# Accumulating layer 1's sums in PSUM, and reading layer 0's attention weights from PSUM

## The chip, the cores and the metric

The kernel runs on one core of a Trainium2 chip, as one launch, in float32. The metric is the device time of the launch in microseconds; lower is better. Five engines work side by side and meet at semaphores: PE (TensorE, matrix multiplies, with PEld for the loading of weights), DVE (VectorE), ACT (ScalarE), POOL (GpSimd) and SP (SyncE, which only issues transfers here). SBUF is the working memory on the chip[...].

## The reference

Two graph layers over 3327 nodes with 512 features; the adjacency matrix has about nine ones in a row. Each layer is added to its input and normalised over the features.

```python
# layer 0: attention with 4 heads of 128 features
feats = jnp.einsum('nf,hfo->hno', X, W)
logits = leaky_relu(e_s[:, :, None] + e_n[:, None, :], 0.2) + NEG_INF * (1.0 - A)
out = relu(einsum('hnm,hmo->hno', softmax(logits), feats) + b)   # heads side by side
x = layernorm(x + out)
# layer 1: a sparse attention and a plain graph convolution, each with a gate
attn_a = sigmoid(concat([adj @ x, x], axis=1) @ Wa.T + ba)       # attn_b with Wb, bb
h = x @ W_sa
e = where(adj != 0, exp(-leaky_relu(s_left[:, None] + s_right[None, :], 0.01)), 0)
x_a = (e / (sum(e, axis=1) + 1e-5)) @ h
x_b = adj @ (x @ W_gcnb) + b_gcnb
x = layernorm(x + sigmoid(attn_a * x_a + attn_b * x_b))
```

The biases are inputs and are added. A second pass over the dense matrix stands behind a branch for inputs that don't fit the sparse lists; it isn't taken here.

## The kernel before

Everything up to about 285 us reads the adjacency matrix, makes for each node the list of its neighbours (up to 24), sorts the nodes by degree into 26 tiles of 128 rows, and writes the rows of layer 0's features to a table in memory. The tiles have 4 to 14 neighbour slots (`CAPS`); the nodes of tiles 0 and 12 that have more share one extra gathered set of rows (`stair`), which two small matrices spread and join (`to_nodes`, L664, and `to_rows`, L676).

Both layers then loop over the 26 tiles. For each tile POOL issues one indirect transfer for each slot (`indirect`, L614, with the instruction on L615): 128 rows of 520 numbers from the table in memory into a ring of 42 slots in SBUF. `plan` lists the gathers of all tiles ahead, and `gather` issues as many as the ring has room for; a tile's slots are given back in `free`, when its readers are done. Other transfers of a loop are few: the scatters of finished rows, L146, also on POOL.

**Layer 0** (loop at L948). `weigh_a` and `weigh_b` make the attention weights of the next tile on DVE and ACT, as `w`, 25 slots by 4 heads. `attend` (L783) multiplies each gathered row by its slot's weights, head by head: DVE for two slots of three (L797, one instruction over 512 numbers, the four weights spread over 128 numbers each), ACT for the third (L795, four instructions). PE adds the rows up in a PSUM bank by multiplying with the identity (L803). `finish` (L883) adds the result to the row, then the norm's statistics follow.

**Layer 1** (loop at L1131). Each turn works on four tiles of the order: `j1` (next; its weights are made), `j` (its rows are summed), `jp` (projected), `jpp` (gated, added and measured). The queues run in the order that the loop writes them (`manual_schedule`), and each engine takes its own instructions in that order:

- `to_sbuf(jp, 1)`, `turn(jp)`, `to_sbuf(jp, 0)`: ACT copies the plain sum of `jp`, which PE has made already transposed (L1098), out of PSUM; PE transposes the weighted sum (L1107); ACT copies that (both copies L1112).
- `plain_sum(j)` on PE, and `weighted(j, 0)` on DVE: the first part of the weighted sum, one SCALAR_TENSOR_TENSOR a slot (L1085): sum = row x weight + sum, the sum `sw` in SBUF, begun by ACT with the tile's own row (`scaled_first`, L1070).
- For `jpp`: DVE adds the bias to the plain projection (L1147), multiplies by the gate and adds the other projection (L1148), and ACT takes the tanh (L1149).
- `project(jp, 1)` and `project(jp, 0)` on PE: the plain and the weighted sum through the two 512x512 matrices (L1118, four matmuls each).
- `weights_a(j1)` (L1032 to L1054), `weighted(j, 1)` (the rest of the slots, and L1087 with the joined rows' sum for tiles 0 and 12), finished rows' norm on ACT (L1161) and their scatters, the residual add of `jpp` (L1171), `weights_b(j1)` (L1059 to L1062), `scaled_first(j1)` (for tiles 0 and 12 with L1073 and the matmul L1075), and the statistics of `jpp` (L692).

Of the kernel before, what the change touches and what calls it, by code (L numbers as in the profile page):

```python
# [8 lines left out]
F32 = mybir.dt.float32  # L9
AF = mybir.ActivationFunctionType  # L10
ALU = mybir.AluOpType
# [13 lines left out]
S = 24  # L25
# [53 lines left out]
def sparse_pass(  # L79
# [104 lines left out]
    def row1(j):  # L184
        g, i = place(j)
        return x1[g][:, i, :]
# [551 lines left out]
        few, many = few[1:], many[1:]  # L738
    order0 += second[-1:]
    assert sorted(order0) == list(range(NT))  # L740
    ws, accs, ws2 = {}, {}, {}

    def weigh_a(j):
        c = slots(j)
# [25 lines left out]
            nc.scalar.copy(ids2[g], stair[j][:, F + H : F + H + 1])  # L770
        nc.scalar.copy(row1(j)[:, 0:F], got[j][0][2][:, 0, 0:F])

    def weigh_b(j):
        c, w = slots(j), ws[j]
        den = m0.tile([P, 1, H], F32, tag="den", name=f"den{j}")
        nc.vector.tensor_reduce(den[:, 0, :], w[:, :c].rearrange("p s h -> p h s"), AX.X, ALU.add)
        nc.vector.reciprocal(den, den)
        nc.vector.tensor_mul(w[:, :c], w[:, :c], den.to_broadcast([P, c, H]))
        if j in T0:
            small = psx.tile([P, B * H], F32, tag="pcol", name=f"to_rows{j}", bufs=2)  # L780
            ws2[j] = to_rows(m0, small, f"n{j}", w[:, C0 + 1 :, :])

    def attend(j, lean, between):  # L783


        w = ws[j]
        acc = accs[j] = ps.tile([P, F], F32, tag="acc", name=f"acc{j}", bufs=2)
        if not lean:
            nc.tensor.matmul(acc, ident, bias0, start=True, stop=False)
        for s0, n, buf, o in got[j]:  # L790
            for s in range(s0, s0 + n):
                gv = buf[:, o + s - s0, 0:F].rearrange("p (h o) -> p h o", h=H)
                if s % 3 == 2:
                    for h in range(H):
                        nc.scalar.activation(gv[:, h, :], gv[:, h, :], AF.Copy, scale=w[:, s, h : h + 1])  # L795
                else:
                    nc.vector.tensor_tensor(  # L797
                        gv, gv, w[:, s, :].rearrange("p (h o) -> p h o", o=1).to_broadcast([P, H, FO]), ALU.mult
                    )
                row = buf[:, o + s - s0, 0:F]  # L800
                if lean and s == 0:
                    nc.vector.tensor_add(row, row, bias0)  # L802
                nc.tensor.matmul(  # L803
                    acc, ident, row, start=(lean and s == 0), stop=(s == CAPS[j] and j not in T0)
                )
                if s == 2:
                    between()
        if j in T0:
            gv = stair[j][:, 0:F].rearrange("p (h o) -> p h o", h=H)
            nc.vector.tensor_tensor(  # L810
                gv, gv, ws2[j].rearrange("p (h o) -> p h o", o=1).to_broadcast([P, H, FO]), ALU.mult
            )
            nc.tensor.matmul(acc, to_node, stair[j][:, 0:F], start=False, stop=True)
# [116 lines left out]
    over = x1b.tile([P, NT, S], F32, name="over")  # L930

    psx = tc.alloc_tile_pool(name="psx", bufs=1, space=PSUM, side="right")
    psum = psx.tile([P, B * H], F32, tag="pcol", name="pv1sum", bufs=2)[:, :NCOL]
    for k in range(KT):
        nc.tensor.matmul(psum, ones, v1[:, k, :], start=(k == 0), stop=(k == KT - 1))
# [78 lines left out]
        order += long[:1] + short[:1]  # L1014
        short, long = short[1:], long[1:]
    order += last
    ew, gates, sums, plain, proj, zs, stair_sum = {}, {}, {}, {}, {}, {}, {}

    def own_score(j):
        ew[j] = m1.tile([P, S + 1], F32, tag="e", name=f"e{j}", bufs=3)  # L1020
        nc.scalar.copy(ew[j][:, 0:1], row1(j)[:, F + 6 : F + 7])

    def weights_a(j):
# [2 lines left out]
        e = ew[j]  # L1026
        gate = gates[j] = m1.tile([P, 12], F32, tag="gate", name=f"gate{j}", bufs=5)
        if j in T0:
            small = ps1.tile([P, B * H], F32, tag="small", name=f"to_nodes1_{j}")
            cols = to_nodes(m1, small, f"l1_{j}", stair[j][:, F : F + 3])  # L1030
        for s0, n, g, _ in got[j]:
            nc.vector.tensor_scalar(e[:, s0 : s0 + n], g[:, :n, F], row1(j)[:, F + 3 : F + 4], None, ALU.add)  # L1032
# [23 lines left out]
    def weights_b(j):  # L1056

        c, e, gate = slots(j), ew[j], gates[j]
        nc.vector.tensor_scalar(gate[:, 2:3], gate[:, 2:3], 1e-5, None, ALU.add)  # L1059
        nc.vector.tensor_scalar(gate[:, 0:2], gate[:, 0:2], 0.5, 0.5, ALU.mult, ALU.add)  # L1060
        nc.vector.reciprocal(gate[:, 2:3], gate[:, 2:3])
        nc.vector.tensor_scalar(e[:, :c], e[:, :c], gate[:, 2:3], gate[:, 0:1], ALU.mult, ALU.mult)  # L1062
        if j in T0:
            small = ps1.tile([P, B * H], F32, tag="small", name=f"to_rows1_{j}")
            ws2[j] = to_rows(m1, small, f"l1_{j}", e[:, C0 + 1 :].rearrange("p (b o) -> p b o", o=1))

    def scaled_first(j):

        sw = sums[j] = m1.tile([P, F], F32, tag="sw", name=f"sw{j}")
        nc.scalar.activation(sw, row1(j)[:, 0:F], AF.Copy, scale=ew[j][:, 0:1])  # L1070
        if j in T0:
            scaled = m1.tile([P, F], F32, tag="scaled", name=f"scaled{j}", bufs=1)
            nc.scalar.activation(scaled, stair[j][:, 0:F], AF.Copy, scale=ws2[j])  # L1073
            stair_sum[j] = ps1.tile([P, F], F32, tag="stair", name=f"stair_sum{j}")
            nc.tensor.matmul(stair_sum[j], to_node, scaled, start=True, stop=True)  # L1075

    def weighted(j, part):

        e, sw = ew[j], sums[j]
        cut = 2 + (CAPS[j] * 5 + 7) // 8  # L1080
        for s0, n, g, _ in got[j]:
            for i in range(n):
                s = s0 + i
                if (s < cut) == (part == 0):
                    nc.vector.scalar_tensor_tensor(sw, g[:, i, 0:F], e[:, s : s + 1], sw, ALU.mult, ALU.add)  # L1085
        if part == 1 and j in T0:
            nc.vector.tensor_add(sw, stair_sum[j], sw)  # L1087

    def plain_sum(j):

# [20 lines left out]
        sT = zs[j, half] = m1.tile([P, KT, P], F32, tag=f"sT{half}", name=f"sT{half}_{j}")  # L1111
        nc.scalar.copy(sT, (turned, plain)[half][j])  # L1112

    def project(j, half):
        sT, wt = zs[j, half], (wsa, wg)[half]
        po = proj[j, half] = ps1.tile([P, F], F32, tag=f"po{half}", name=f"po{half}_{j}", bufs=1 + half)
        for k in range(KT):
            nc.tensor.matmul(po, sT[:, k, :], wt[:, k, :], start=(k == 0), stop=(k == KT - 1))  # L1118

    ends = {3, 7, 11, 15, 19, 22, 24, 25}  # L1120
    norm = Norm(m1, "n1", ends)
# [9 lines left out]
    for i in range(NT + 3):  # L1131
# [3 lines left out]
        gather()  # L1135
        if j1 is not None:
            own_score(j1)
        if jp is not None:
            to_sbuf(jp, 1)
            turn(jp)  # L1140
            to_sbuf(jp, 0)
        if j is not None:
            plain_sum(j)
            weighted(j, 0)
        if jpp is not None:
            za = zs[jpp] = m1.tile([P, F], F32, tag="za", name=f"za{jpp}", bufs=3)
            nc.vector.tensor_add(za, bias_g, proj[jpp, 1])  # L1147
            nc.vector.scalar_tensor_tensor(za, za, gates[jpp][:, 1:2], proj[jpp, 0], ALU.mult, ALU.add)  # L1148
            nc.scalar.activation(za, za, AF.Tanh, scale=0.5)  # L1149
        if jp is not None:  # L1150
            project(jp, 1)
            project(jp, 0)
        if j1 is not None:
            weights_a(j1)
        if j is not None:
# [16 lines left out]
        if j1 is not None:  # L1172
            weights_b(j1)
            scaled_first(j1)
        if jpp is not None:
            ready = norm.add(i - 2, zs[jpp])

# [451 lines left out]
```

## Time and profile before

| what | value |
|---|---|
| median of 3 runs | 1068.92 us (1057.76 to 1071.53) |
| the profiled execution's own time | 897.77 us |
| its span, first to last instruction | 895.8 us |
| mean granted clock of TensorE | 0.908 |
| layer 0's loop | about 285 to 527 us |
| layer 1's first and last gather, issued at | 530.94 and 842.26 us |
| PE's last projection ends | 879.8 us |

A line of the groups is: source line, engine, operation, output<-inputs, shapes, count | busy us, mean ns of one | idle us of the engine just before them, and what ended it. The chain that ended last is followed back from the last instruction to what released each one. PE's clock is granted in full or by half, by the profile's rows. The profiled execution is shorter than the timed runs by 171 us.

### The profile page before, as it was taken

How to read it: one execution, taken by the hardware profiler on the slowest of the kernel's cores; microseconds unless marked ns; L12 is line 12 of the kernel's file. 1: busy time of each engine (PE TensorE's matmuls, PEld its weight loads, DVE VectorE, ACT ScalarE, POOL GpSimd, SP SyncE). 2: the span in 40 equal slices, each digit the busy share in tenths (PEclk: the TensorE clock that was granted, in tenths of full speed). 3: DMA queues.
4: the chain of work that ended last, by engine and by line, in shares of the span. 5: the costliest groups of instructions: out<-in, count | busy, mean ns of one | idle time of the engine just before them, and what ended most of it. 6: DMA issues, size and time to landing. Idle time of an engine off the chain costs nothing. (4 is left out here: it accounts for less than half of the span.)

```text
span 895.8 us, 11378 instructions
## 1 busy us (share of the span) xinstructions
PE 745.3 (83%) x3118; PEld 457.4 (51%) x3118; DVE 693.3 (77%) x2032; ACT 272.0 (30%) x794; POOL 595.2 (66%) x641
## 2 busy tenths in 40 slices
PE   4698997416799978799999957987997999999992
PEld 3477775103445534344444435654764666666551
DVE  4288787896678858769898845957996999998973
ACT  0122221002335525444646512212222222232231
POOL 6711133566577777777777747777777777777772
PEclk9799999556899989889999967999898999999997
DMA  8989999999777878789777637677767777777641
GB/s 330 369 340 403 366 377 345 380 387 399 267 225 227 276 234 263 231 278 329 219 234 228 222 115 203 188 199 201 187 184 196 192 196 195 203 193 199 195 187 74
DMA packets 73352, 224.74 MB, mean 251 GB/s; under 512 B 12736, under 2 KB 16784, under 8 KB 72384
## 3 DMA queue, kind: packets, MB, share of 16 engines
q0 software_dynamic: 46368, 153.69, 56.9%
q1 hardware_dynamic: 24256, 68.13, 19.9%
q10 hardware_dynamic: 2656, 2.10, 0.7%
q8 instruction: 27, 0.44, 0.2%
q14 instruction: 45, 0.37, 0.1%
HBM read 203.02 MB, written 31.51 MB: 262 GB/s over the span
## 5 line engine op out<-in xcount | busy, mean ns | idle before, releaser
L615 POOL DMA_INDIRECT ring<-table,srt x464 | 475.7, 1025 | 162.1 <-issue 56.2
L803 PE MATMUL acc<-ring,ident 128*128 128x512 f32 x504 | 239.4, 619 | 18.9 <-DVE ring L802 12.9
L1085 DVE SCALAR_TENSOR_TENSOR sw<-ring,e,sw 128x512 f32<-128x512 f32 x226 | 169.8, 751 | 10.7 <-ACT sw L1070 4.2
L803 PEld LDWEIGHTS acc<-ring,ident 128*128 128x128 f32 x504 | 94.4, 196 | 130.3 <-issue 74.3
L371 PE MATMUL pf<-w,xc 128*128 128x260 f32 x416 | 102.9, 410 | 13.1 <-DVE w L311 13.1
L1098 PE MATMUL acc<-ident,ring 128*128 128x128 f32 x904 | 108.6, 280 | 6.2 <-DMA ring<-table,srt 6.1
L797 DVE TENSOR_TENSOR ring<-ring,w 128x512 f32<-128x512 f32 x176 | 111.8, 693 | 0.5
L1098 PEld LDWEIGHTS acc<-ident,ring 128*128 128x128 f32 x904 | 103.6, 145 | 8.1 <-DMA ring<-table,srt 8.1
L1118 PE MATMUL po<-wsa,sT 128*128 128x512 f32 x208 | 95.4, 602 | 4.6 <-DVE za L1148 2.3
L371 PEld LDWEIGHTS pf<-w,xc 128*128 128x128 f32 x416 | 84.1, 205 | 29.3 <-DVE w L311 13.8
L1118 PE MATMUL po<-wg,sT 128*128 128x512 f32 x208 | 93.6, 593 | 0.0
L795 ACT ACTIVATE ring<-ring,w 128x128 f32<-128x128 f32 x304 | 91.5, 390 | 0.0
L383 POOL DMA_DIRECT2D table<-row x26 | 14.2, 549 | 85.2 <-ACT st L380 82.6
L1118 PEld LDWEIGHTS po<-wsa,sT 128*128 128x128 f32 x208 | 39.7, 193 | 56.6 <-issue 56.1
L1118 PEld LDWEIGHTS po<-wg,sT 128*128 128x128 f32 x208 | 37.5, 190 | 37.3 <-issue 37.3
L1149 ACT ACTIVATE za<-za 128x512 f32<-128x512 f32 x26 | 16.4, 630 | 127.7 <-DVE za L1148 127.7
L402 PE MATMUL pc<-at,pow 128*32 128x512 bf16 (+1 forms) x182 | 23.3, 413 | 35.3 <-DMA at<-in_adjB 25.4
L762 ACT ACTIVATE w<-w 128x40 f32<-128x40 f32 (+10 forms) x26 | 6.2, 237 | 127.5 <-DVE w L761 127.5
L375 ACT COPY row<-pf 128x512 f32<-128x512 f32 x26 | 15.2, 586 | 95.4 <-PE pf L371 49.7
L834 PEld LDWEIGHTS pcol<-v,xt 128*128 128x128 f32 x208 | 28.7, 201 | 14.5 <-issue 12.1
L828 ACT COPY xt<-x1t 128x512 f32<-128x512 f32 x26 | 15.2, 584 | 62.9 <-PE x1t L822 62.9
L402 PEld LDWEIGHTS <-pow 128*32 128x32 bf16 x182 | 7.3, 97 | 47.9 <-issue 44.8
(252 smaller groups left out, 918.4 us busy)
## 6 DMA issues: line engine op xcount, KB each, us to landing
at<-in_adjB SPq DMA_DIRECT2D x78, 512.0 KB, 11.5
ring<-table,srt POOLq DMA_INDIRECT x464, 3.9
table<-row POOLq DMA_DIRECT2D x26, 260.0 KB, 6.1
xc<-in_xB SPq DMA_DIRECT2D x6, 1024.0 KB, 8.4
own<-in_xo SPq DMA_DIRECT2D x1, 3640.0 KB, 46.5
own<-table SPq DMA_DIRECT2D x1, 3640.0 KB, 55.2
at<-in_adjL SPq DMA_DIRECT2D x13, 256.0 KB, 9.9
table<-in_xo SPq DMA_DIRECT2D x1, 3120.0 KB, 27.2
```

Source lines behind the costliest of these rows:

```text
L371: nc.tensor.matmul(pf[:, hh, :HC], xc[:, k, o : o + P], w0[:, k, hh, :], start=(k == 0), stop=(k == KT - 1))
L375: nc.scalar.copy(row[:, 0:F].rearrange("p (h o) -> p h o", h=2), pf[:, :, 0 : F // 2])
L402: nc.tensor.matmul(pc[32 * c : 32 * c + 32, : nt * P], pow2[:, s, :], loaded[i, m], start=(s == 0), stop=(m + 1 not in ms or s == 3),)
L615: return nc.gpsimd.indirect_dma_start(out=out_, out_offset=None, in_=table, in_offset=bass.IndirectOffsetOnAxis(ap=ap, axis=0)).ins
L795: nc.scalar.activation(gv[:, h, :], gv[:, h, :], AF.Copy, scale=w[:, s, h : h + 1])
L797: nc.vector.tensor_tensor(gv, gv, w[:, s, :].rearrange("p (h o) -> p h o", o=1).to_broadcast([P, H, FO]), ALU.mult)
L803: nc.tensor.matmul(acc, ident, row, start=(lean and s == 0), stop=(s == CAPS[j] and j not in T0))
L834: nc.tensor.matmul(pcol, xt1[:, k, :], v1[:, k, :], start=(k == 0), stop=(k == KT - 1))
L1085: nc.vector.scalar_tensor_tensor(sw, g[:, i, 0:F], e[:, s : s + 1], sw, ALU.mult, ALU.add)
L1098: nc.tensor.matmul(pl[:, k, :], row[:, k * P : (k + 1) * P], to_node if steps else ident, start=(i + k == 0), stop=(i == len(rows) - 1 and ...
L1118: nc.tensor.matmul(po, sT[:, k, :], wt[:, k, :], start=(k == 0), stop=(k == KT - 1))
L1149: nc.scalar.activation(za, za, AF.Tanh, scale=0.5)
```

## The change

In layer 0, a bank of PSUM (`wps`) holds the attention weights of three tiles; DVE copies each tile's weights there, and DVE's multiplies read them from it. ACT's multiplies and the joined rows go on reading `w` in SBUF.

In layer 1 four things are kept in PSUM and added up there:

- `so_far`, the weighted sum, is begun by ACT in a bank of PSUM and carried on there by DVE; the last slot's instruction writes the sum to SBUF (`sw`). The cut between the two parts is limited so that the last slot falls in the second.
- `gated`, one bank: ACT writes the bias into it (`plain_done`), the plain projection is added to it by PE (no instruction starts the sum anew), and ACT multiplies it by the gate into another bank.
- `zas`, two banks in turn: ACT's product stands there, PE adds the weighted projection, and ACT takes the tanh from it. L1147 and L1148 on DVE are gone.
- The loop's order: the tanh of `jpp` and the plain projection of `jp` come at the front of a turn, ahead of `turn(jp)`; the bias copy and the copy of the plain sum of `j` come near the end of the turn before, behind `scaled_first(j1)`. Three matmuls with the identity put the bias into the three banks once.

To make room, the joined rows' three small results share one bank (`small`). The number of transfers and their order on each queue stay.

```diff
+    def in_psum(j):
+
+        return wps[0][:, order0.index(j) % 3, :].rearrange("p (s h) -> p s h", h=H)
+
     def weigh_b(j):
...
         nc.vector.tensor_mul(w[:, :c], w[:, :c], den.to_broadcast([P, c, H]))
+        nc.vector.tensor_copy(in_psum(j)[:, :c], w[:, :c])
...
     def attend(j, lean, between):
-        w = ws[j]
+        w, wp = ws[j], in_psum(j)
...
                     nc.vector.tensor_tensor(
-                        gv, gv, w[:, s, :].rearrange("p (h o) -> p h o", o=1).to_broadcast([P, H, FO]), ALU.mult
+                        gv, gv, wp[:, s, :].rearrange("p (h o) -> p h o", o=1).to_broadcast([P, H, FO]), ALU.mult
                     )
...
+    wps.append(psx.tile([P, 3, (S + 1) * H], F32, name="wps"))
...
     def scaled_first(j):
-        sw = sums[j] = m1.tile([P, F], F32, tag="sw", name=f"sw{j}")
-        nc.scalar.activation(sw, row1(j)[:, 0:F], AF.Copy, scale=ew[j][:, 0:1])
+        so_far[j] = ps1.tile([P, F], F32, tag="so_far", name=f"so_far{j}")
+        nc.scalar.activation(so_far[j], row1(j)[:, 0:F], AF.Copy, scale=ew[j][:, 0:1])
...
     def weighted(j, part):
-        e, sw = ew[j], sums[j]
-        cut = 2 + (CAPS[j] * 5 + 7) // 8
+        e, sw = ew[j], so_far[j]
+        if part == 1:
+            sums[j] = m1.tile([P, F], F32, tag="sw", name=f"sw{j}")
+        cut = min(2 + (CAPS[j] * 5 + 7) // 8, CAPS[j])
...
-                    nc.vector.scalar_tensor_tensor(sw, g[:, i, 0:F], e[:, s : s + 1], sw, ALU.mult, ALU.add)
+                    to = sums[j] if s == CAPS[j] else sw
+                    nc.vector.scalar_tensor_tensor(to, g[:, i, 0:F], e[:, s : s + 1], sw, ALU.mult, ALU.add)
         if part == 1 and j in T0:
-            nc.vector.tensor_add(sw, stair_sum[j], sw)
+            nc.vector.tensor_add(sums[j], stair_sum[j], sums[j])
...
-    def project(j, half):
+    gated = ps1.tile([P, F], F32, name="gated")
+    zas = [ps1.tile([P, F], F32, name=f"za{n}") for n in range(2)]
+    for to in (gated, *zas):
+        nc.tensor.matmul(to, ident, bias_g, start=True, stop=True)
+
+    def project(n, j, half):
+
         sT, wt = zs[j, half], (wsa, wg)[half]
-        po = proj[j, half] = ps1.tile([P, F], F32, tag=f"po{half}", name=f"po{half}_{j}", bufs=1 + half)
+        po = gated if half else zas[n % 2]
         for k in range(KT):
-            nc.tensor.matmul(po, sT[:, k, :], wt[:, k, :], start=(k == 0), stop=(k == KT - 1))
+            nc.tensor.matmul(
+                po, sT[:, k, :], wt[:, k, :], start=False, stop=(k == KT - 1), skip_group_check=True
+            )
+        if half:
+            nc.scalar.activation(zas[n % 2], gated, AF.Copy, scale=gates[j][:, 1:2])
+
+    def plain_done(j):
+
+        nc.scalar.copy(gated, bias_g)
+        to_sbuf(j, 1)
...
+        if jpp is not None:
+            za = zs[jpp] = m1.tile([P, F], F32, tag="za", name=f"za{jpp}", bufs=3)
+            nc.scalar.activation(za, zas[i % 2], AF.Tanh, scale=0.5)
         if jp is not None:
-            to_sbuf(jp, 1)
+            project(i - 1, jp, 1)
             turn(jp)
             to_sbuf(jp, 0)
         if j is not None:
             plain_sum(j)
             weighted(j, 0)
-        if jpp is not None:
-            za = zs[jpp] = m1.tile([P, F], F32, tag="za", name=f"za{jpp}", bufs=3)
-            nc.vector.tensor_add(za, bias_g, proj[jpp, 1])
-            nc.vector.scalar_tensor_tensor(za, za, gates[jpp][:, 1:2], proj[jpp, 0], ALU.mult, ALU.add)
-            nc.scalar.activation(za, za, AF.Tanh, scale=0.5)
         if jp is not None:
-            project(jp, 1)
-            project(jp, 0)
+            project(i - 1, jp, 0)
...
         if j1 is not None:
             weights_b(j1)
             scaled_first(j1)
+        if j is not None:
+            plain_done(j)
```

More of the change, by code (lines that the diff above doesn't have):

```diff
@@ L740, in sparse_pass @@
     assert sorted(order0) == list(range(NT))
-    ws, accs, ws2 = {}, {}, {}
+    ws, accs, ws2, wps = {}, {}, {}, []
     def weigh_a(j):
@@ L1016, in sparse_pass @@
     order += last
-    ew, gates, sums, plain, proj, zs, stair_sum = {}, {}, {}, {}, {}, {}, {}
+    ew, gates, sums, plain, proj, zs, stair_sum, so_far = {}, {}, {}, {}, {}, {}, {}, {}
     def own_score(j):
@@ L1028, in weights_a @@
         if j in T0:
-            small = ps1.tile([P, B * H], F32, tag="small", name=f"to_nodes1_{j}")
+            small = ps1.tile([P, F], F32, tag="small", name=f"to_nodes1_{j}")
             cols = to_nodes(m1, small, f"l1_{j}", stair[j][:, F : F + 3])
@@ L1063, in weights_b @@
         if j in T0:
-            small = ps1.tile([P, B * H], F32, tag="small", name=f"to_rows1_{j}")
+            small = ps1.tile([P, F], F32, tag="small", name=f"to_rows1_{j}")
             ws2[j] = to_rows(m1, small, f"l1_{j}", e[:, C0 + 1 :].rearrange("p (b o) -> p b o", o=1))
     def scaled_first(j):
-        sw = sums[j] = m1.tile([P, F], F32, tag="sw", name=f"sw{j}")
-        nc.scalar.activation(sw, row1(j)[:, 0:F], AF.Copy, scale=ew[j][:, 0:1])
+        so_far[j] = ps1.tile([P, F], F32, tag="so_far", name=f"so_far{j}")
+        nc.scalar.activation(so_far[j], row1(j)[:, 0:F], AF.Copy, scale=ew[j][:, 0:1])
         if j in T0:
@@ L1073, in scaled_first @@
             nc.scalar.activation(scaled, stair[j][:, 0:F], AF.Copy, scale=ws2[j])
-            stair_sum[j] = ps1.tile([P, F], F32, tag="stair", name=f"stair_sum{j}")
+            stair_sum[j] = ps1.tile([P, F], F32, tag="small", name=f"stair_sum{j}")
             nc.tensor.matmul(stair_sum[j], to_node, scaled, start=True, stop=True)
     def weighted(j, part):
-        e, sw = ew[j], sums[j]
-        cut = 2 + (CAPS[j] * 5 + 7) // 8
+        e, sw = ew[j], so_far[j]
+        if part == 1:
+            sums[j] = m1.tile([P, F], F32, tag="sw", name=f"sw{j}")
+        cut = min(2 + (CAPS[j] * 5 + 7) // 8, CAPS[j])
         for s0, n, g, _ in got[j]:
```

## The prediction

> **What bounds the kernel now.** I read the page first, then the table by stretches, the groups of instructions, the chain that ended last and a timeline of two tiles of layer 1. No engine is full over the span:
>
> ```profile
> PE 745.3 (83%) x3118; PEld 457.4 (51%) x3118; DVE 693.3 (77%) x2032; ACT 272.0 (30%) x794; POOL 595.2 (66%) x641
> ```
>
> By stretches (columns: busy us of PE, PEld, DVE, ACT, POOL, then the granted clock, DMA share, GB/s) it looks different. Layer 0's loop runs from about 285 to 527 us, layer 1's from 531 to the end:
>
> ```profile
> 400.00:500.00 100.00, 96.95 (x307) 47.86 (x307) 84.11 (x232) 52.98 (x159) 76.30 (x78) 1.00 0.82 254
> 600.00:700.00 100.00, 86.43 (x448) 59.91 (x447) 83.69 (x199) 24.80 (x62) 78.38 (x72) 0.93 0.70 191
> 700.00:800.00 100.00, 100.00 (x505) 65.81 (x504) 93.39 (x212) 27.88 (x72) 77.77 (x74) 1.00 0.72 195
> ```
>
> In layer 1 PE is full at full clock from 700 to 800 us, with DVE at 93 beside it. POOL reads 78, but it is full too: in the timeline a gather follows each gather with a gap of 0.30 us and nothing more, from 530.94 to the last one at 842.26. These are 230 gathers, (842.26 - 530.94)/229 = 1.36 us from one to the next. So three engines are within a few per cent of each other, and relief of one of them is worth only what the next one leaves. The groups (busy us, mean ns, then idle before):
>
> ```profile
> L615 POOL DMA_INDIRECT ring<-table,srt x228 | 243.4, 1067 | 71.7 <-issue 19.9 <-DMA ring<-table,srt 14.9 <-PE acc L1098 13.4
> L1085 DVE SCALAR_TENSOR_TENSOR sw<-ring,e,sw 128x512 f32<-128x512 f32 x226 | 169.8, 751 | 10.7 <-ACT sw L1070 4.2 <-ACT e L1021 0.3
> L1148 DVE SCALAR_TENSOR_TENSOR za<-za,gate,po 128x512 f32<-128x512 f32 x26 | 19.4, 747 | 5.9 <-PE po L1118 3.5
> L1147 DVE TENSOR_TENSOR za<-bias_g,po 128x512 f32<-128x512 f32 x26 | 17.6, 679 | 0.0
> L1171 DVE SCALAR_TENSOR_TENSOR x1b<-za,x1b 128x512 f32<-128x512 f32 x14 | 9.6, 686 | 1.5 <-ACT za L1149 1.4
> L885 DVE SCALAR_TENSOR_TENSOR x1b<-acc,x1b 128x512 f32<-128x512 f32 x14 | 9.5, 679 | 3.6 <-PE acc L813 3.4 <-PE acc L803 0.2
> L797 DVE TENSOR_TENSOR ring<-ring,w 128x512 f32<-128x512 f32 x176 | 111.8, 693 | 0.5
> ```
>
> The timeline shows why a gather's mean is 1067 ns, when those beside an idle DVE take 0.94 to 0.95 us (start, length):
>
> ```profile
> 704.14 4.72 DVE L1085 SCALAR_TENSOR_TENSOR sw<-ring,e,sw 128x512 f32<-128x512 f32 x6
> ...
> 706.83 1.27 POOL L615 DMA_INDIRECT ring<-table,srt  x1 [0.30 <-PE po L1118]
> ...
> 709.55 0.75 DVE L1148 SCALAR_TENSOR_TENSOR za<-za,gate,po 128x512 f32<-128x512 f32 x1
> ...
> 709.97 0.95 POOL L615 DMA_INDIRECT ring<-table,srt  x1 [0.30 <-PE acc L1098]
> ```
>
> Beside L1085, which takes both of its tensors from SBUF, a gather stretches to 1.27 us; beside L1148, one of whose tensors lies in PSUM, it does not. The chain shows where DVE's work after the projections still reaches PE:
>
> ```profile
> 616.27 0.77 DVE sw L1085
> 617.05 0.75 DVE sw L1085
> 617.81 0.61 DVE za L1147
> 618.51 0.76 DVE za L1148
> 619.40 3.67 PE po L1118 x8
> ```
>
> **The change, part by part.**
>
> *1. DVE loses L1147 and L1148*: 26 x 679 + 26 x 747 ns = 17.6 + 19.4 = 37 us, 1.4 us a tile. The residual add (L1171) stays, and so do the norms. One copy of the bias through PE per bank (3 matmuls of about 0.9 us) is issued between 529.1 and 534.2 us, where PE waits for layer 1's first gathers: nothing.
>
> *2. ACT gains two 128x512 instructions a tile*: PSUM to PSUM with a scale, and the bias into PSUM. No row writes PSUM from ACT. Nearest rows: L1112, a copy out of PSUM, 575 to 586 ns, and L1070, with a scale from SBUF, 719 ns. So 26 x 2 x 0.58 to 0.72 = 30 to 37 us (taken: 33), on an engine that is 28% busy from 700 to 800. What matters is who waits. PE's first projection of a tile now stands in front of the transposes of the sum and waits for ACT's copy of the plain sum, which stands last in ACT's turn of the loop, behind the first scaled row (which waits for DVE's weights). From the start S of PE's turn, for an average tile: projection to S+3.4, ACT scale to S+4.1, copy of the transposed sum to S+4.75, exponential and gate to S+5.4, DVE's weights (L1059 to L1062, 0.95) to S+6.3, scaled row to S+7.1, bias to S+7.7; the plain sum ends on PE at S+8.3, its copy at S+8.9. The next turn begins at S+11.7 (0.44 + 4.4 + 6.87). So 2.8 us of cover: nothing, as long as DVE isn't over 2.8 us late. Before the two tiles with joined rows PE waits anyway, and the 2 us matmul of L1075 covers the two copies.
>
> *3. The 226 L1085 keep their count, but accumulate in PSUM*; the last one of each tile writes SBUF. Reading PSUM costs nothing by the rows: 679 (L885) against 686 (L1171), 747 (L1148) against 751 (L1085). Writing PSUM from DVE has no row. [...] I take 750 ns, unchanged[...]. [...]
>
> *4. POOL*: if a PSUM operand ends the stretch, gathers go to 946 + 300 ns. Layer 1: 230 x (1.36 - 1.25) = 25 us. Layer 0: by the page all 464 take 475.7 us, so its 236 take 232.3, 984 each, and 236 x 0.038 = 9 us go. [...] the rows (1.27 against 0.95) show it held. I take the rows.
>
> *5. Layer 0*: 26 small copies into PSUM; the nearest row is L838, 151 to 156 ns: +4.0 us of DVE. The 176 multiplies, with one input streamed from PSUM: [...]taken 680, so -2.3 us. DVE is then 1.7 us longer under a PE that is 97% busy there: nothing. Faster gathers help where DVE waited for rows (2.3 us before L749 at 497.7 us): -2.
>
> *What reaches the end.* PE's work does not shrink, so only its pauses in layer 1 count; from 546 to 880 us there are about 27 us (half-clock spells among them). 617.1 to 619.4 waits for L1148: 2.3, gone. 834.1 to 836.0, and the projection behind it at half clock (5.4 instead of 3.4): 3.9, gone, since DVE is 1.4 us and the gathers 1 us a tile ahead by then. 590.3 to 594.5 waits for rows landing at 592.9: half of it, 2.1. The waits for the two tiles with joined rows (5.7 and 7.2 us) are a round trip PE, DVE, PE, ACT, PE that stays; the two za instructions leave it: 2.4. Behind the last projection ACT can start at once: 1.4. Sum for layer 1: 12.1, with layer 0: 14.
>
> The profiled execution took 897.8 us (span 895.8), the runs' median is 1068.9, 19% more. Nothing in the page says where those 171 us are. If they are apart from the loops, 14 us stay 14; if everything stretches, they are 17. So 1069 - 16 = 1053.
>
> **The rivals.**
>
> *A, as worked out (chance 0.50)*: 1053, own range 1035 to 1065; about 0.22 of it lies beyond 2% faster (under 1047.5).
>
> *D, gathers set the pace in the timed runs (0.17)*: the full stretch is 464 x (1.27 - 0.95) = 148 us, of which the profiled execution has 464 x (1025 - 946) = 37. If half of the other 111 is in the 171, the change takes it away with the 14: 1069 - 70 = about 1000. For it: POOL never pauses in either loop. Against: POOL would have to be hit by far more of the same DVE instructions.
>
> *B, hidden anyway (0.11)*: if PE runs at a lower clock in the timed runs (745 us x 0.908 = 677 us at full clock; with the 151 us of span in which it isn't busy, 1069 needs 677/918 = 0.74), PE has no pauses left for anything to fill, and the gain is 0 to 3 us: 1067. That is also the rival in which the gathers' stretch isn't ended by the operand.
>
> *C, slower (0.22)*: DVE's chain through PSUM is slower. Each L1085 reads what the one before wrote; they follow at 0.786 us. It decides at 37/226 = 0.16 us: over 0.95 us a step DVE has lost what L1147 and L1148 gave, its weights come late, and PE's first projection waits behind ACT's queue. At 0.2 us: 45 - 37 = +8 in layer 1; with 0.1 us for the 176 multiplies, +18 on DVE in layer 0, of which the 16% that DVE is idle hides about half: +9. With the late first projections (0.4 us x 20 tiles) +25: 1094. Against it: rows L885 and L1148.
>
> **How the numbers follow.** Beyond 2% is about what a measurement of this kernel can tell from no change (the runs differ by 1.3%). Faster by over 2%: 0.22 of A and D: 0.39. Within: 0.28 of A, 0.11 of B, 0.03 of C: 0.42. Slower: 0.19 of C. For 8 in 10 the range leaves out D's lower half and C's upper half: 1006 to 1092.
>
> **What would show it.** Right: gathers at 0.95 us in both loops and the last one about 20 us earlier; L1085's successor at about 750 ns, following at 0.79; no pause of PE in front of the first projection between 700 and 800; span near 882. Wrong: the successor at 820 ns or more, or multiplies in layer 0 over 750 (C); gathers still at 1.07 (POOL's part fails); PE waiting on ACT's copy at each tile (part 2 fails).

## The result, and the profile after

The changed kernel is slower: 1112.85 us (median of 4 runs, 1101.56 to 1115.14) against 1066.88 us for the kernel before (4 runs, 1057.76 to 1071.53), a ratio of 1.046 (95% interval 1.038 to 1.055). The prediction said 1053 and a range of 1006 to 1092. The ratios in this text are those on record, which use the runs in the fast state alone and differ from the quotients of the medians by up to 0.6% (1.043 here).

Both kernels run in one of two conditions, which I call short and long: in the short one the kernel before takes 897 us, in the long one 1067 us. The condition came with a session on a chip and not with the chip (one chip was met in both), and within a session it held for every kernel. The execution that the page of before shows (897.8 us) was short; its timed runs, those of after, and the trace of after are long. Every ratio here compares runs of one condition, taken side by side.

In the long condition (profile of after, engines of the whole span, and three stretches with the columns of the table shown of before: layer 0, the start of layer 1, the middle of layer 1):

```profile
PE 794.3 (71%) x3124; PEld 469.5 (42%) x3124; DVE 662.5 (60%) x2006; ACT 300.2 (27%) x846; POOL 558.2 (50%) x641
```

```profile
400.00:500.00 100.00, 76.87 (x218) 37.88 (x216) 61.10 (x196) 34.05 (x106) 61.27 (x64) 0.86 0.74 230
640.00:740.00 100.00, 52.85 (x210) 30.41 (x211) 41.76 (x98) 19.37 (x50) 60.70 (x64) 0.72 0.63 173
850.00:950.00 100.00, 73.03 (x343) 46.92 (x344) 65.49 (x153) 28.05 (x66) 52.40 (x56) 0.86 0.53 147
```

No engine is full any more, in either loop. PE, which was at 100% of 700 to 800 us, is at 73, and the granted clock at 0.86. The same changed kernel in the short condition (run e10) looks as the prediction's page did:

```profile
400.00:500.00 100.00, 96.65 (x309) 47.89 (x308) 85.62 (x238) 54.22 (x162) 75.92 (x80) 1.00 0.84 264
600.00:700.00 100.00, 89.46 (x466) 61.09 (x465) 74.58 (x185) 32.32 (x75) 75.68 (x80) 0.93 0.77 213
700.00:800.00 100.00, 100.00 (x520) 67.25 (x519) 87.31 (x205) 38.58 (x92) 75.75 (x80) 1.00 0.77 213
```

Here DVE fell from 93 to 87 and PE did 520 matmuls in 100 us for 505 before. So the stages, from the traces (us; layer 0 from its first sum on PE, which stands ahead of its loop, to its last; layer 1 from there to its last projection):

| kernel, condition | up to layer 0 | layer 0 | layer 1 |
|---|---|---|---|
| before, short (5 traces) | 214 to 216 | 303 to 307 | 357.4 to 360.6 |
| after, short (e10) | 215.4 | 305.6 | 354.3 |
| after, long (the result) | 243.3 | 374.9 | 479.2 |
| after, long (e5) | 248.8 | 378.5 | 476.0 |
| layer 1's change alone, long (e6) | 244.0 | 371.5 | 465.3 |
| only the order changed, long (e13) | 235.6 | 376.2 | 448.7 |
| after with the old cover, long (e14) | 250.1 | 374.5 | 452.0 |
| sum and layer 0 in PSUM, old order, long (e18) | 232.6 | 373.5 | 443.0 |

From short to long every stage grows: for after by 28, 69 and 125 us, which with the end are the 222 us between the spans (890.3 and 1112.2). Layer 0 differs by 7 us at most among the long traces, and layer 1 by 36.

The stage ahead of layer 0, which the change does not touch, differs too, by 17 us among the long traces (232.6 to 250.1). The traces run alike up to about 180 us: PE's last matmul of L402 ends between 178.9 and 184.8 us in all of them. ACT's last L416, which waits for it, starts within 0.1 us of it in the short traces and at 198 to 218 us in the six long ones, each with a wait of 28 to 33 us (the waits of before, short, then of after, long: us in total, times, longest):

```profile
ACT v L416 <- PE pc L402: 52.3, 14, 10.0
```

```profile
ACT v L416 <- issue: 33.1, 1, 33.1
```

So some of a difference between two long traces can lie where their code is the same.

The groups of after that answer to those shown of before (busy us, mean ns, then idle before):

```profile
L615 POOL DMA_INDIRECT ring<-table,srt x464 | 443.7, 956 | 332.8 <-issue 105.8 <-PE acc L1107 69.2 <-PE acc L808 46.7
L1094 DVE SCALAR_TENSOR_TENSOR so_far<-ring,e,so_far 128x512 f32<-128x512 f32 x200 | 151.0, 755 | 16.3 <-ACT so_far L1076 4.8
L1133 PE MATMUL gated<-wg,sT 128*128 128x512 f32 x208 | 115.2, 705 | 87.1 <-ACT sT L1121 47.5 <-issue 39.6
L802 DVE TENSOR_TENSOR ring<-ring,wps 128x512 f32<-128x512 f32 x176 | 109.3, 681 | 0.6
L1094 DVE SCALAR_TENSOR_TENSOR sw<-ring,e,so_far 128x512 f32<-128x512 f32 x26 | 19.4, 746 | 1.7
L1137 ACT ACTIVATE za<-gated,gate 128x512 f32<-128x512 f32 x26 | 17.2, 662 | 91.1 <-PE gated L1133 56.9 <-PE acc L1107 12.7 <-issue 9.0
L1121 ACT COPY sT<-acc 128x512 f32<-128x512 f32 x26 | 15.2, 584 | 117.7 <-remote 98.5 <-PE acc L1107 12.1 <-PE za L1133 7.2
L1141 ACT COPY gated<-bias_g 128x512 f32<-128x512 f32 x26 | 14.9, 571 | 0.0
```

Line numbers are those of the changed kernel: L1094 is the old L1085, L802 the old L797, L1133 the old L1118, L1121 the old L1112. Instruction durations are as the prediction took them. The news is in two idle columns: ACT waits 117.7 us in front of its copy of the plain sum, and PE 87.1 us in front of the plain projection that reads this copy (both 0.0 in the profile of before). In the short condition, e10, the same two groups:

```profile
L1133 PE MATMUL gated<-wg,sT 128*128 128x512 f32 x208 | 99.6, 624 | 10.5 <-ACT sT L1121 10.5
L1121 ACT COPY sT<-acc 128x512 f32<-128x512 f32 x26 | 15.1, 582 | 15.8 <-PE acc L1107 15.5
```

The timeline shows what happens in such a turn. Short condition (e10), a tile with 48 transposes of rows:

```profile
661.62 5.40 PE L1107 MATMUL acc<-ident,ring 128*128 128x128 f32 x48
665.12 0.57 ACT L1141 COPY gated<-bias_g 128x512 f32<-128x512 f32 x1
666.86 3.60 PE L1133 MATMUL za<-wsa,sT 128*128 128x512 f32 x8
667.06 0.59 ACT L1121 COPY sT<-acc 128x512 f32<-128x512 f32 x1 [1.37 <-PE acc L1107]
670.29 3.60 PE L1133 MATMUL gated<-wg,sT 128*128 128x512 f32 x8
```

And a turn with 48 in the long condition (after):

```profile
821.51 5.40 PE L1107 MATMUL acc<-ident,ring 128*128 128x128 f32 x48
...
824.85 0.57 ACT L1141 COPY gated<-bias_g 128x512 f32<-128x512 f32 x1
826.75 3.60 PE L1133 MATMUL za<-wsa,sT 128*128 128x512 f32 x8
831.16 0.94 POOL L615 DMA_INDIRECT ring<-table,srt  x1 [0.30 <-PE za L1133]
835.42 0.59 ACT L1121 COPY sT<-acc 128x512 f32<-128x512 f32 x1 [10.00 <-remote]
```

The last transpose ends at the same distance from the burst's start (5.40 us), and ACT is free behind the bias copy in both. Short: the copy starts 0.04 us behind the transposes. Long: 8.5 us behind them, and no instruction that ended shortly before is on record as its releaser ("remote"). PE has 3.6 us of other work, and then stands.

The trace's records of PE's semaphore, for which this copy waits, show that it was not ACT's own queue that was held. In e10 they stand 0.43 to 0.44 us apart from 662.23 to 667.04 us, 0.02 us before the copy. In after they stand at 824.48, 825.23, 828.11 and 831.00, and then four times between 835.28 and 835.49: the updates came late, and in a clump. PE's ends are modelled in these profiles, so the trace can't tell a late update from a burst that ended late; PE's next projection had begun at 826.75.

Over the 26 tiles, leaving out the first and the two with joined rows, the copy comes at most 1.1 us behind the last row in the short condition; in the long one 41.9, 13.7, 12.4, 9.5, 9.4, 8.5, 7.3, 4.3, 3.8 and 3.0 us behind it in ten tiles. Part of this is ACT's own work: of the 41.9 us, 33.2 lie behind the end of both PE's burst and ACT's instruction before. Behind the longest PE waits 29.8 us, and the chain of after runs through it:

```profile
667.35 0.69 ACT so_far L1076
668.04 0.51 ACT gated L1141
668.55 33.17 another core or an unknown queue
701.71 0.02 issue
701.74 0.59 ACT sT L1121
702.33 0.04 issue
702.38 5.67 PE gated L1133 x8
```

The last line shows a second price: after a pause the eight matmuls take 5.67 us for 3.60. The granted clock (behind the busy time in a table of stretches of PE alone) had fallen to 0.50 while PE stood, and is 0.64 in these matmuls:

```profile
702.40:708.00 5.60, 5.60 (x10) 0.64 0.37 106
...
690.00:701.70 11.70, 0.00 (x0) 0.50 0.32 90
```

Over the kernel that is 705 ns a matmul of L1133's plain half, for 624 in the short condition.

### The profile page after: what moved, and what is told of

Read it like the earlier page. It is cut to its first block, busy times and chain, and to the rows that moved or that the text cites. A ratio compares the mean times of both kernels' runs of the same rounds, so it can differ in the third digit from the quotient of the medians.

```text
span 1112.2 us, 11360 instructions
## 1 busy us (share of the span) xinstructions
PE 794.3 (71%) x3124; PEld 469.5 (42%) x3124; DVE 662.5 (60%) x2006; ACT 300.2 (27%) x846; POOL 558.2 (50%) x641
## 5 line engine op out<-in xcount | busy, mean ns | idle before, releaser
L615 POOL DMA_INDIRECT ring<-table,srt x464 | 443.7, 956 | 332.8 <-issue 105.8
L808 PE MATMUL acc<-ring,ident 128*128 128x512 f32 x504 | 259.9, 665 | 67.1 <-DVE ring L807 34.9
L1133 PE MATMUL gated<-wg,sT 128*128 128x512 f32 x208 | 115.2, 705 | 87.1 <-ACT sT L1121 47.5
L1094 DVE SCALAR_TENSOR_TENSOR so_far<-ring,e,so_far 128x512 f32<-128x512 f32 x200 | 151.0, 755 | 16.3 <-ACT so_far L1076 4.8
L1133 PEld LDWEIGHTS gated<-wg,sT 128*128 128x128 f32 x208 | 46.7, 230 | 155.1 <-issue 102.8
L802 DVE TENSOR_TENSOR ring<-ring,wps 128x512 f32<-128x512 f32 x176 | 109.3, 681 | 0.6
L1133 PE MATMUL za<-wsa,sT 128*128 128x512 f32 x208 | 97.4, 608 | 7.9 <-issue 7.1
L1133 PEld LDWEIGHTS za<-wsa,sT 128*128 128x128 f32 x208 | 38.3, 195 | 47.2 <-issue 46.1
L383 POOL DMA_DIRECT2D table<-row x26 | 14.3, 551 | 84.1 <-ACT st L380 81.4
L402 PE MATMUL pc<-at,pow 128*32 128x512 bf16 (+1 forms) x182 | 23.7, 417 | 33.4 <-DMA at<-in_adjB 23.5
L1121 ACT COPY sT<-acc 128x512 f32<-128x512 f32 x26 | 15.2, 584 | 117.7 <-remote 98.5
L1137 ACT ACTIVATE za<-gated,gate 128x512 f32<-128x512 f32 x26 | 17.2, 662 | 91.1 <-PE gated L1133 56.9
```

The costliest lines, as they stand in the source:

```text
L402: nc.tensor.matmul(pc[32 * c : 32 * c + 32, : nt * P], pow2[:, s, :], loaded[i, m], start=(s == 0), stop=(m + 1 not in ms or s == 3),)
L615: return nc.gpsimd.indirect_dma_start(out=out_, out_offset=None, in_=table, in_offset=bass.IndirectOffsetOnAxis(ap=ap, axis=0)).ins
L802: nc.vector.tensor_tensor(gv, gv, wp[:, s, :].rearrange("p (h o) -> p h o", o=1).to_broadcast([P, H, FO]), ALU.mult)
L808: nc.tensor.matmul(acc, ident, row, start=(lean and s == 0), stop=(s == CAPS[j] and j not in T0))
L1094: nc.vector.scalar_tensor_tensor(to, g[:, i, 0:F], e[:, s : s + 1], sw, ALU.mult, ALU.add)
L1133: nc.tensor.matmul(po, sT[:, k, :], wt[:, k, :], start=False, stop=(k == KT - 1), skip_group_check=True)
```

## The experiments

The first expectations name five theories. **O**: the new order costs its time wherever it runs. **T**: each added wait between engines costs. **M**: PSUM operands make DVE slower. **S**: in the timed runs engines start late behind a semaphore. **P**: the prediction's sums hold in the short condition. From e7 on there are two. **L**: the new order loses its cover. The copy of the plain sum waits for PE's signal, and between the plain sum and the projection that needs the copy PE now has one projection (3.4 us); before it had two, a transposition and the next plain sum (about 12 us). **G**: the sums in PSUM cost it, through DVE or ACT's added instructions. The prediction's own rival C is a form of G.

**The parts, in the short condition.** e1 is the kernel before; e2 has layer 0's part alone; e3 the weighted sum in PSUM alone; e4 gate, bias and projections in PSUM with the new order, and the sum in SBUF.

```diff
# e2: layer 0 only
+        nc.vector.tensor_copy(in_psum(j)[:, :c], w[:, :c])
# e3: sum only (old order, L1147 and L1148 kept)
-        sw = sums[j] = m1.tile([P, F], F32, tag="sw", name=f"sw{j}")
+        so_far[j] = ps1.tile([P, F], F32, tag="so_far", name=f"so_far{j}")
# e4: gates only
+        po = gated if half else zas[n % 2]
...
-            to_sbuf(jp, 1)
+            project(i - 1, jp, 1)
```

> The kernel before, unchanged, for a trace under the conditions of the timed runs. If the 171 us between the profiled execution and the timed runs are a property of the conditions (theory S: engines start late after a semaphore, in waits that no work explains), this trace spans about 1065 us, with the same busy time per engine as before (PE near 745 us, DVE near 693) and long pauses in front of waiting instructions, some of 10 to 30 us. If not, it spans 897 again. Ratio 1.00.

> Layer 0's part of the change alone. Theory O (the order of layer 1's loop costs the 46 us: the first projection waits for ACT's copy behind DVE's weights): ratio 0.99 to 1.00 here. Theory T (every wait on another engine costs more in the timed runs, so each added link costs wherever it is; here one copy of about 0.15 us a tile, on DVE alone, without a new engine): 1.00 to 1.01. Theory M (PSUM operands of DVE cost time): 1.01 to 1.02 with multiplies over 693 ns.

> The running sum of layer 1 in PSUM alone, with the joined rows' three results in one bank; gates, projections and order as before. Theory O: 0.98 to 1.00 (gathers no longer stretched beside DVE, nothing else moved). Theory M: 1.01 to 1.03. Theory T: 1.00.

> The gated sum in PSUM and the new order of layer 1's loop alone; the weighted sum stays in SBUF and layer 0 as before. Theory O and theory T: most of the 4.6%, 1.03 to 1.06, with PE pausing in front of the first projection of each turn (L1133 gated) for 2 to 4 us a tile. Theory M: 0.99 to 1.00.

Measured: e1 896.5 us (1.0003, 0.9985 to 1.0021), and with it the first sight of the short condition in timed runs; e2 1.0013 (0.9992 to 1.0033); e3 0.9935 (0.9916 to 0.9953); e4 1.0008 (0.9991 to 1.0025). Only the sum gains; M had expected a loss of e3 (1.01 to 1.03), O and T one of e4 (1.03 to 1.06), and in this condition neither came. S had nothing to be tested on here. POOL's busy time from 530 to 880 us shows by what; e3, then a kernel before (e15):

```profile
530.00:880.00 350.00, 243.03 (x253) 0.94 0.68 194
```

```profile
530.00:880.00 350.00, 269.91 (x253) 0.96 0.69 192
```

The same 253 instructions take 27 us less. In the timeline of e3 each gather beside L1088 (e3's L1085) takes 0.94 to 0.95 us:

```profile
647.38 7.09 DVE L1088 SCALAR_TENSOR_TENSOR so_far<-ring,e,so_far 128x512 f32<-128x512 f32 x9
647.44 0.95 POOL L615 DMA_INDIRECT ring<-table,srt  x1 [0.30 <-DVE mvn L693]
648.69 0.94 POOL L615 DMA_INDIRECT ring<-table,srt  x1 [0.30 <-PE po L1121]
```

e4 takes 33 us of busy time from DVE (693.8 in e1, 660.4 in e4; the two groups' 37 us overlap their neighbours by the rest) and gives ACT 31 (271.8 to 302.5), and the time stays. The order alone costs 0.3 to 0.6% in this condition (e8 and e11, below), so DVE's relief may have bought that back; more it did not.

**The change again, in the long condition.** e5 is the changed kernel, e6 the same with layer 0 as before.

> The changed kernel itself, timed beside the kernel before in the condition in which the kernel before takes 897 us. Theory P (the sums of the prediction hold there, and the 4.6% belong to the other condition): 0.98 to 0.99, span near 880. Theory O (the new order of the loop costs 46 us wherever it runs): 1.03 to 1.05. The four kernels before this one took 1.000, 1.001, 0.9935 and 1.001, which leaves for O only that the parts hurt together.

> The whole change of layer 1, layer 0 as before. Theory P: 0.985 to 0.995, within 0.3% of the changed kernel, since layer 0's part alone took 1.001. Theory O: as the changed kernel, 1.03 to 1.05. If the chip is in the condition of 1067 us, the changed kernel and this one show which layer holds the 4.6%.

Measured: e5 1107.3 against 1072.0 us, 1.035 (1.027 to 1.043); e6 1.032 (1.025 to 1.039). Both lie in O's range (1.03 to 1.05), and the loss comes with layer 1's part of the change, to within these intervals. P speaks of the short condition and was not tested by them.

**The order by itself, and one turn more of cover.** e8 is the kernel before with nothing changed but the place of two calls. e9 is the changed kernel with its PSUM sums, in the old order of turn, plain sum and projection; what followed from them comes one turn later.

```diff
# e8: order only, on the kernel before
-            to_sbuf(jp, 1)
+            project(jp, 1)
             turn(jp)
...
-            project(jp, 1)
             project(jp, 0)
...
             scaled_first(j1)
+        if j is not None:
+            to_sbuf(j, 1)
# e9: one turn later, on the changed kernel
-            project(i - 1, jp, 1)
+            to_sbuf(jp, 1)
             turn(jp)
...
-            project(i - 1, jp, 0)
+            project(i - 1, jp, 1)
+        if jpp is not None:
+            project(i - 2, jpp, 0)
```

> The kernel before once more, for its trace. Chips differ: it took 897 us on one and 1072 on another. On a chip of the second kind theory L (PE's signal to the other engines comes late there after a long burst of transposes, by 8 to 14 us after 48 rows or more) expects late copies L1112 of the plain sum here too, hidden by some 12 us of PE's work between the burst and the projection that needs the copy; PE pauses in front of L1118 are then short. Ratio 1.00.

> The kernel before with only the order of layer 1 changed: the plain projection of a tile stands at the front of the next turn, and ACT's copy of the plain sum at the end of its own turn; sums, bias and gate as before. On a chip of 1067 us: theory L expects 1.02 to 1.05, with PE pausing 5 to 10 us in front of L1118 behind tiles of 11 slots and more; theory G (ACT's two added instructions a tile and the sums in PSUM cost it) expects 0.99 to 1.00. On a chip of 897 us: both 0.99 to 1.01.

> The changed kernel with the loop's order mended: transposes, plain sum and plain projection in the order of the kernel before, and the weighted projection, the tanh and the residual one turn later, so that neither ACT's copy nor its gate stands between two steps of PE in one turn. All sums in PSUM as in the changed kernel. On a chip of 1067 us: theory L expects 0.97 to 1.00 of the kernel before; theory G 1.03 to 1.05 as the changed kernel. On a chip of 897 us: theory L 0.975 to 0.99, theory G 0.99 to 1.00.

> The changed kernel again, on the same chip as the three others. On a chip of 1067 us: 1.035 to 1.05, with the pauses of PE in front of L1133. On a chip of 897 us theory L expects 0.985 to 0.995 (the sums of the prediction, smaller than there), theory O (the order costs wherever it runs) 1.03 or more.

Measured, all in the short condition: e7 0.9995 (0.9977 to 1.0013); e8 1.0026 (0.9995 to 1.0058); e9 0.988 (0.982 to 0.994); e10, the changed kernel, 0.991 (0.988 to 0.995). So the change that loses 4.6% in one condition gains 0.9% in the other, within the 0.985 to 0.995 expected of e10, and O (1.03 or more wherever it runs) falls. With the old cover it gains 1.2%, which the intervals don't tell from 0.9. What the order costs where the change loses had to be seen in the long condition, with the same kernels:

> The order alone once more, since its first runs fell on a chip of 897 us (1.003 there). On a chip of 1067 us: theory L (PE's signal comes late behind a long burst of transposes, and the new order leaves 3.4 us of cover in place of some 12) 1.02 to 1.05; theory G (ACT's added instructions and the sums in PSUM) 0.99 to 1.00. On a chip of 897 us again 1.00.

> The kernel before, for its trace on the same chip. On a chip of 1067 us theory L expects ACT's copies of the plain sum (L1112) 8 to 14 us behind the last transpose of tiles with 11 slots or more, and little pause of PE in front of L1118; where that is not so, L falls. On a chip of 897 us: copies within 1 us of the time when ACT is free.

> The order alone a third time: on chips of 897 us it took 1.003 and 1.006. On a chip of 1067 us theory L expects 1.02 to 1.05, theory G 0.99 to 1.01.

> The sums in PSUM with the plain projection behind the plain sum and the weighted projection one turn later, again: 0.988 on a chip of 897 us. On a chip of 1067 us theory L expects 0.97 to 1.00, theory G 1.03 to 1.05.

e11 and e12 were short once more: 1.0056 (1.0039 to 1.0073) and 1.0013 (0.9997 to 1.0029). e13 and e14 were long: the order alone costs 1.020 (1.012 to 1.027), and the changed kernel with the old cover 1.018 (1.009 to 1.028), where e5 has 1.035. e13 lies at the lower edge of L's range and outside of G's; e14 lies between the two ranges, so it was a miss for both. The order's traces, first long (e13), then short (e11), with the numbers of the kernel before:

```profile
L1118 PE MATMUL po<-wg,sT 128*128 128x512 f32 x208 | 116.2, 711 | 81.4 <-issue 74.3 <-ACT sT L1112 7.0
L1112 ACT COPY sT<-acc 128x512 f32<-128x512 f32 x26 | 15.1, 581 | 118.4 <-remote 94.3 <-PE po L1118 18.9 <-PE acc L1098 5.0
```

```profile
L1118 PE MATMUL po<-wg,sT 128*128 128x512 f32 x208 | 97.5, 612 | 15.3 <-ACT sT L1112 15.3
L1112 ACT COPY sT<-acc 128x512 f32<-128x512 f32 x26 | 14.7, 566 | 0.3 <-PE acc L1098 0.3
```

e13 has no sum in PSUM and no added instruction on ACT, and yet ACT waits 118.4 us for the plain sum and PE 81.4 in front of the projection: the pause comes with the order. The late signal does not. e18, the last kernel below, has the old order, and in its long trace ACT waits 89.4 us in front of the same copy, while PE hardly pauses in front of the projection:

```profile
L1127 PE MATMUL po<-wg,sT 128*128 128x512 f32 x208 | 103.4, 639 | 2.9 <-issue 2.9
L1121 ACT COPY sT<-acc 128x512 f32<-128x512 f32 x26 | 15.1, 581 | 89.4 <-remote 73.8 <-PE acc L1107 10.1 <-PE po L1127 5.6
```

So the signal is late under either order, and the cover decides whether PE stands for it. With the cover back in the changed kernel (e14) PE's pause is gone; ACT comes to this copy 7.4 us or more behind the transposes there and doesn't wait:

```profile
L1133 PE MATMUL gated<-wg,sT 128*128 128x512 f32 x208 | 98.0, 615 | 2.2 <-ACT sT L1121 1.9 <-issue 0.3
L1121 ACT COPY sT<-acc 128x512 f32<-128x512 f32 x26 | 15.1, 580 | 0.0
```

But 85 us of pauses went, and only some 1.7% (18 us) of the time, by intervals that just meet. In layer 1's stage the traces differ by 13 to 27 us (452.0 in e14, 465.3 to 479.2 in e6, e5 and the result); e14's has lost most of all ahead of layer 0 (250.1), which the order does not touch. Part of the pauses had only changed place: in every long trace PE has one slow stretch of 30 to 40 us early in layer 1. In after it stands before the projection (29.8 us at 673), in e13 too (36.2 at 660), in e14 among the transposes.

**The rest: the sum in PSUM.** The order explains 2.0% of 3.5 to 4.6. The last four kernels are for what remains: e15 is before (for its trace in the long condition), e16 is e3, e17 is e4, and e18 has the two parts that leave the order alone, e2's and e3's edits together.

> The kernel before, unchanged. If this run falls in the long condition (before at about 1067 us), its trace has layer 0 at about 375 us, as every kernel there, and the stretch from layer 1's first plain sum to its last projection at about 420 to 430 us. Theory L (late completion signal; in before's order some 12 us of PE's work lie over it): ACT's copy of the plain sum comes just as late behind PE's end (8 to 30 us in places) but PE's pauses in front of L1118 come to under 40 us, against the 86 us in front of L1133 in the changed kernel. Rival G (the signals are late only in the changed kernel, because of its PSUM sums): no copy comes over 3 us late. In the short condition (897 us) it tells nothing new: 0.998 to 1.002.

> Only the weighted sum in PSUM, with before's order of the loop and L1147, L1148 kept. In the long condition theory L expects no loss, since the order has its cover: 0.985 to 1.005. Rival G (the sums in PSUM cost what the order does not explain, 4.6% less 2.0%): 1.015 to 1.03. In the short condition 0.9935 again, within 0.003.

> Layer 1's gate, bias and projections in PSUM with the new order; the weighted sum stays in SBUF, layer 0 as before. In the long condition (before at about 1067 us) theory L, in which the order and ACT's added instructions make the loss, expects the whole of what layer 1's change costs there: 1.025 to 1.04, with PE's pauses in front of L1133's counterpart (the gated projection) of over 60 us. Rival G, in which the sums in PSUM make the rest, expects no more than the order alone: 1.012 to 1.025. In the short condition it repeats 1.0008 (0.998 to 1.004).

> Two of the three parts: layer 0's weights in PSUM and the weighted sum in PSUM; the order, the bias, the gate and both projections stay as before (L1147 and L1148 included). If the parts add up, the short condition (before at about 897 us) gives 0.9934 + 0.0013 = 0.9947 (0.992 to 0.997). In the long condition (about 1067 us) theory L (loss by the order, and by ACT's instructions in the way of the projection) expects no loss: 0.985 to 1.005; rival G (the sum in PSUM makes what the order doesn't explain) 1.015 to 1.03.

e15 to e17 were short: 0.9992 (0.9972 to 1.0011), 0.9932 (0.9909 to 0.9955), 1.0017 (0.9999 to 1.0035); they repeat the parts and tell nothing of the rest. e18 was long: 1077.4 against 1066.7 us, 1.013 (1.003 to 1.023). This speaks against **theory L alone**, which expected no loss (0.985 to 1.005), but doesn't decide: G expected 1.015 to 1.03, and the interval reaches into both ranges. Nor can the trace show the loss: the execution that it records took 1066.87 us, as much as the median of the kernel before. PE hardly waits in front of its first projection, as shown; its slow stretch of PE, 648 to 690 us, looks like this:

```profile
653.47 1.01 PE L1127 MATMUL po<-wsa,sT 128*128 128x512 f32 x1 [2.22 <-DVE so_far L1094]
656.26 1.01 PE L1127 MATMUL po<-wsa,sT 128*128 128x512 f32 x1 [1.78 <-issue]
659.06 1.01 PE L1127 MATMUL po<-wsa,sT 128*128 128x512 f32 x1 [1.79 <-issue]
661.86 0.37 PE L1116 MATMUL pt<-ident,sw 128*128 128x128 f32 x1 [1.79 <-issue]
664.66 0.37 PE L1116 MATMUL pt<-ident,sw 128*128 128x128 f32 x1 [2.43 <-issue]
```

One matmul every 2.80 us, of 1.01 or 0.37 us each, nearly all waiting for nothing recorded ("issue"). As e13 has no sum in PSUM and e18 not the new order, and both have such a stretch, neither part is needed for it.

Put together, in the long condition: order 2.0% (e13) and sum with layer 0 1.3% (e18) make 3.3%, and layer 1's change as a whole is 3.2% (e6), the whole change 3.5% (e5) and 4.6% (the result). The parts add up, but their intervals together reach from 1.5 to 5.0%, so this says little. In the short condition the same parts are +0.3 to +0.6% (e8, e11) and -0.7% (e3, e16).

## Why the prediction was wrong, by its own steps

**What bounds the kernel.** Right for the execution that the page shows and for the short condition (e10: PE 100, DVE 87, gathers every 1.25 us); it does not hold for the timed runs. The prediction saw the gap of 171 us and let it be "apart from the loops" or a stretch of everything in proportion. It was neither: from short to long, the changed kernel's layer 0 grows by 69 us of 306 and layer 1 by 125 of 354, and PE is no longer full in either. The sum of pauses was taken from an execution that the timed runs did not have.

**Part 1, DVE's 37 us.** Right in size: both groups are gone. The time of e4 is unchanged, and against the order alone (e8, e11) that is a gain of some 0.2 to 0.5%: relief of one of three engines was worth little, as the first part of the prediction has it.

**Part 2, "2.8 us of cover: nothing, as long as DVE isn't over 2.8 us late".** This is the step that failed, as far as the loss is explained. ACT's instructions cost what was taken (662 and 571 ns, together 32 us; 33 taken), DVE was not later than before (ACT waits 30 us for its weights in front of the scaled rows, for 51 in the page of before), and in the short condition the cover held: PE pauses once before the projection, for 10.5 us at the loop's start (e10). The prediction watched for DVE and ACT; what came late was PE's own signal, by the records of its semaphore and by 3 to 33 us beyond the end of PE's burst and of ACT's work, more than a cover of 2.8 us. Moving the copy from a place with some 12 us of PE's work behind it to one with 3.4 was priced at nothing, and in the long condition it is 2.0% (1.2 to 2.7, e13), of a loss of 3.5 (e5) to 4.6. The cause of the rest stays open.

**Part 3, L1085 through PSUM.** Right: 755 ns in PSUM, 746 for the last one, against 751 in SBUF; 681 against 693 in layer 0 (680 taken, near L1147's 679). With this **rival C** falls, although it alone stood on the side where the time went: its chain on DVE is not slower. Its addition, late first projections at 0.4 us x 20 tiles, named the place by another cause and a tenth of the size.

**Part 4, gathers.** Right: over both loops 956 ns in after and 961 in e10, for 1025 in the page of before, and in e3 27 us less on POOL from 530 to 880 us (25 predicted for layer 1). The last gather is issued at 818.87 us in e10, 23 us earlier than in the page of before (about 20 predicted). Beside DVE's L1085, with both tensors in SBUF, a gather took 1.27 us; beside its successor with the sum in PSUM 0.94 to 0.95 (e3). How the one held the other these rows don't show. **Rival D** falls: in the long condition the stretch is no greater (a mean of 1014 ns over both loops in e13, whose L1085 and layer 0 are the old ones, against 1025).

**Part 5, layer 0.** -2 us predicted; 1.0013 (0.9992 to 1.0033) measured, so nothing that can be told.

**The sum of 14 us.** In the short condition the change is worth 0.9% of 897, 8 us (5 to 10), where the prediction had 14 on that execution. In layer 1's stage 12 us were counted, and 3 to 6 came (354.3 for 357.4 to 360.6), and the new order alone costs some 2 to 5 us of the whole time (e8, e11), which the sum had at nothing. **Rival B** is half right on the clock (0.84 to 0.86 granted in the long runs, the kernel before among them, against 0.908) and wrong in what follows, as PE has more pauses there (87.1 us before the plain projection, 10.5 in e10) and not none.

## What stays open

Why the long condition exists, and why PE's signal is late in it. The traces of that condition hold 7,100 to 7,600 records of semaphore updates for about 14,400 in the short one. Up to 100 us they have as many as the short ones (about 1,500), between 175 and 200 us 41 to 68 for 415 to 475, and there the first long wait stands. So recording is itself disturbed, and it can't be told from these traces whether the recording slows the engines or suffers with them. Nor is PE the only one: in after DVE, in a row of instructions that each wait for DVE's own one before, starts three instructions of L71 and L74 at 184.63, 187.43 and 190.24 us, 2.80 us apart, and such three in the short trace e15 at 173.94, 174.66 and 175.15 us. Whether the sum in PSUM, which gains 0.7% in the short condition, is what loses 1.3% (0.3 to 2.3) in the long one: e18 has the part of layer 0 with it, and no trace of the kernel before was caught in the long condition to set beside it. Whether the sum alone loses there wasn't measured. And of the 4.6% of the result about 1.3 lies above the sum of the parts; the result's interval and that of e5 overlap, so it may be scatter.

## What to carry to other kernels

Before a sum of microseconds is made, compare the profiled execution's own time with the timed runs. If they differ by far more than the runs do among themselves (here 171 us, the runs of before 14), the page shows another condition, and a wait read from it as covered need not be covered in the runs. A copy that waits for another engine's long burst is best placed with the most work of that engine between the burst and the copy's reader: it cost nothing that can be told where the signal is prompt (e9: 0.988 with it, e10: 0.991 without), and where it is late the order is a part of the price (e13, the order alone: 1.020; e14: 1.018 with the cover, e5: 1.035 without). And a stage that a change does not touch is worth a look first: what two traces differ by there, their other stages may differ by too. No version that was timed in both conditions beats the kernel before in both; the sum alone (e3) was never timed in the long one.

## What was not expected of the hardware

One kernel has two conditions 19% apart (897 and 1067 us). Each held through a session, with runs within 1.3% of each other in the short one and up to 3.2% in the long (before, beside e5). In the long one the records of PE's semaphore, and the copy that waits for them, come late behind bursts of transposes: in after 8.5 us behind 48 of them in 5.4 us, and 3.0 to 41.9 us in ten of 23 tiles; about 1 us at most in the short condition (e10). ACT waits for it under either order (118.4 us in e13, 89.4 in e18). PE (e18) and DVE (after) step at times through single instructions 2.80 us apart. With the weighted sum in PSUM the gathers beside DVE's sum take 0.94 to 0.95 us (e3) for 1.27 (before), and the mean of POOL's 253 instructions from 530 to 880 us is 961 ns (e3) for 1067 (e15), at no cost to DVE (755 ns for 751).
